# Moving the small updates of a top-k search and of the softmax sums from VectorE to GpSimd inside an attention stage

## The chip, the cores and the metric

The kernel runs on one core of a Trainium2 chip. The metric is the device time of one execution in microseconds (us), the median of three runs. The engines are named as the profile names them: PE (TensorE, matmul), PEld (its weight load), DVE (VectorE), ACT (ScalarE), POOL (GpSimd) and SP (SyncE, which here only issues DMAs). Each engine executes its own queue in order, and engines wait for each other through semaphores.

## The reference, cut to what matters

Two transformer-like layers on x of shape (4, 32, 32, 384). The change lies in the attention of layer 0:

```python
attn = softmax(einsum('bhnd,bhmd->bhnm', q, k) * scale)      # 4 x 12 heads, 1024 x 1024
gidx = argmax(einsum('bhnd,hgd->bhng', q, gp))               # 48 groups a head
q_mean = mean of q over the tokens of each group             # b h 48 32
qmw_t = einsum('bhgd,bhnd->bhgn', q_mean, k)
mask = the 96 largest of the 1024 values of each row of qmw_t
col = mask.sum(axis=2)                                       # how many groups chose token m
attn = attn * col[..., None, :]
attn = attn / (attn.sum(axis=2, keepdims=True) + 1e-08)      # normalised over the queries
out = einsum('bhnm,bhmd->bhnd', attn, v) @ proj_w.T
```

So a head needs, for each query n, the inverse of its sum of exponentials; for each key m, `col`; and then a second normalisation along the other axis. After attention come an expert feed-forward, a local attention and a second feed-forward, which the change does not touch.

## The kernel before, in words

All of attention is written as one loop over `step` (L889), with four steps to a head and 48 heads, 192 steps and ten more to drain. A step handles two of the eight blocks of 128 keys. The order of instructions on PE, DVE, ACT and SP is the order of the Python text; on POOL, which is not in that list, the compiler's scheduler chooses the order. Stages of one head are spread over steps:

- `scores(u)` (L649): four pairs of matmuls of a 32-row `k4` block with `q4` into two PSUM tiles `ps_s` (two buffers, so the next step's scores wait for this step's `exps`).
- `exps` (L659, ACT): two exponentials of 128 x 1024 to SBUF tiles `e`.
- `total(u)`, one step later (L667, `ps_z`): sums of exponentials over the keys, by matmul with ones.
- `gather`, when a head's four steps are over: ACT copies the sums (L681), SP writes them to DRAM (L683) and reads them back as `zz`, 128 x 2 x 8 (L685).
- `spread`, in step 1 of the next head: DVE adds the two halves (L693) and takes the reciprocal (L695); SP writes that to DRAM (L697) and reads it back repeated over all partitions as `rz` (L699). For the last head of an image three more DVE instructions (L703 to L705) check that the sums lie within bounds.
- `share(u)`, `SHARE` = 7 steps after the scores (L711, DVE): two instructions of 128 x 1024 multiply `e` by `rz` and by `inv` and sum along the row; then L716 and L718 make the scaled values `wv`.
- `out(u)`, `OUT` = 8 steps after the scores (L667, `ps_o`): the product with `wv`. `keep` copies it to SBUF (ACT, L731) and sends it to its place in `q`: SP writes one half (L740), POOL adds the other by an accumulating DMA (L738).
- `Head(n + 1)` is created in step 0 of head n and at once issues eight DMAs on POOL's queue, L636 and L637 in turn, that fill `q4` and `k4` (two buffers each).

Between these, `prepared` puts projections and grouping of the next image on PE, `project` and `residue` put the output projection of the image before, and `search` runs the top-k search. A search (`topk`, 20 tiles of up to 128 rows, two of them at a time) finds a bound by iteration: ACT counts how many of the 1024 values lie above the bound with a Sign and a running sum (L384 for the first size, then L391 eight times), and between two counts DVE makes the new bound from the count (L395, L397). After the last, DVE negates it (L401) and takes the largest values below (L404 to L425). Sign writes its unneeded output into `junk`, which is the same memory as `below`, the tile that L404 writes. A search advances by one part each time `search()` is called, twice in a step, after `share` and `spread`.

`residue` (L764, SP) loads the input row block that the output projection is added to, into `o`, a tile with one buffer until attention is over; L782 adds, L783 to L786 take statistics, L787 stores.

Of the kernel before, what the change touches and what calls it, by code (L numbers as in the profile page):

```python
# [10 lines left out]
FP = mybir.dt.float32  # L11
BF = mybir.dt.bfloat16
AF = mybir.ActivationFunctionType
ALU = mybir.AluOpType
# [3 lines left out]
P = 128  # L18
B, IMG, C = 4, 32, 384
NTOK = IMG * IMG  # L20
NB = NTOK // P
# [16 lines left out]
FIRST_BOUND, NEAR, SLOPE = 1.65, 92, 0.00366  # L38
DAMP = (0.9, 0.7, 0.5, 0.4, 0.3, 0.25, 0.2)
# [137 lines left out]
def attention(net, outer, router, x, x1, unsafe, qkv_wT, gpT, proj_wT, proj_w, gate_w, gate_b):  # L177
# [14 lines left out]
    tc, nc = net.tc, net.nc  # L192
    NHEAD = B * NH
# [6 lines left out]
    few = outer.enter_context(tc.tile_pool(name="at_few", bufs=2))  # L200
    psum = router.psum
    with ExitStack() as ctx:

        early = ctx.enter_context(tc.tile_pool(name="at_early", bufs=1))
        const = ctx.enter_context(tc.tile_pool(name="at_const", bufs=1))
# [3 lines left out]
        tiny = ctx.enter_context(tc.tile_pool(name="at_tiny", bufs=4))  # L209
# [40 lines left out]
        for t in range(5):  # L250
            for n in range(4):
                one = hsel[:, t, n : n + 1]
                lo = NG * (FIRST[t] + n) - P * t
                nc.gpsimd.affine_select(
                    out=one, in_=one, compare_op=ALU.is_ge, fill=0.0,
                    base=-lo, pattern=[[0, 1]], channel_multiplier=1,
                )
                nc.gpsimd.affine_select(
                    out=one, in_=one, compare_op=ALU.is_ge, fill=0.0,
                    base=lo + NG - 1, pattern=[[0, 1]], channel_multiplier=-1,  # L260
                )
        ones16 = const.tile([P, TOPK], BF, name="ones16")
        nc.gpsimd.memset(ones16, 1.0)
        nc.gpsimd.memset(qmbd, 0.0)
# [9 lines left out]
        nc.gpsimd.memset(topped[:, 0, :], 1.0)  # L274
        nc.gpsimd.memset(topped[:, 1, :], float(2 * TOPK - NTOK))
        below = const.tile([P, 512], FP, name="below")
        junk = below.bitcast(mybir.dt.bfloat16)
        fit = const.tile([P, B], FP, name="fit")
        onehot = const.tile([P, B * KC * NB // 2], FP, name="onehot")
        sums = lasting.tile([P, NE], FP, name="sums")  # L280
# [44 lines left out]
        reached, heads, projected, valued = set(), [], set(), set()  # L325
# [38 lines left out]
        def topk(b, t):  # L364
# [10 lines left out]
            n = rows_of(t)  # L375
            left = load(b, t)
            yield
            size = small("tk_size")
            parts = tiny.tile([P, 51], FP, name="tk_parts", tag="tk_parts", bufs=2)
            step, place, last, none, between = (parts[:, c : c + 1] for c in range(5))  # L380
# [3 lines left out]
            nc.scalar.activation(junk[:n], left[:n], AF.Abs, accum_out=size[:n])  # L384
            yield
            bound = small("tk_bound")
            nc.vector.tensor_scalar(bound[:n], size[:n], -FIRST_BOUND / NTOK, None, ALU.mult)
            for turn in range(len(DAMP) + 1):
                yield
                over = small("tk_over")  # L390
                nc.scalar.activation(junk[:n], left[:n], AF.Sign, bias=bound[:n], accum_out=over[:n])  # L391
                yield
                if turn == len(DAMP):
                    break
                nc.vector.scalar_tensor_tensor(step[:n], over[:n], float(NTOK - 2 * NEAR), size[:n], ALU.add, ALU.mult)  # L395
                old, bound = bound, small("tk_bound")
                nc.vector.scalar_tensor_tensor(  # L397
                    bound[:n], step[:n], -SLOPE * DAMP[turn] / NTOK, old[:n], ALU.mult, ALU.add
                )
            edge = best[:, 0:1]  # L400
            nc.vector.tensor_scalar(edge[:n], bound[:n], -1.0, None, ALU.mult)  # L401
            for half in range(2):
                cols = slice(half * 512, half * 512 + 512)
                nc.vector.scalar_tensor_tensor(  # L404
# [216 lines left out]
        class Head:  # L621
            def __init__(self, n):
                self.n, self.b, self.h = n, n // NH, n % NH
                self.c, self.j = self.h // 4, self.h % 4
                self.rows = slice(32 * self.j, 32 * self.j + 32)
                self.im = images[self.b]
                assert (self.b, self.c, "qk") in reached

                self.q4 = big.tile([P, 512], FP, name="q4", tag="q4", bufs=2)
                self.k4 = big.tile([P, 512], FP, name="k4", tag="k4", bufs=2)  # L630
                q = self.im["q"][self.c][self.rows, :]
                k = self.im["k"][self.c][self.rows, :].rearrange("p (a e t) -> p a e t", e=2, t=P)
                for r in range(4):
                    rows_ = slice(32 * r, 32 * r + 32)
                    odd, half = divmod(r, 2)
                    nc.gpsimd.dma_start(out=self.q4[rows_, :], in_=q[:, 512 * half : 512 * half + 512])  # L636
                    nc.gpsimd.dma_start(  # L637
                        out=self.k4[rows_, :].rearrange("p (a t) -> p a t", t=P), in_=k[:, :, odd, :]
                    )
                self.es = []  # L640
                self.s = tiny.tile([P, NB], FP, name="s", tag="s")

            def scores(self, u):
                self.ps = []
# [45 lines left out]
            def spread(self):  # L690

                z = self.im["z"][:, self.h, :]
                nc.vector.tensor_tensor(z, self.zz[:, 0, :], self.zz[:, 1, :], ALU.add)  # L693
                rr = tiny.tile([P, NB], FP, name="rr", tag="rr", bufs=2)
                nc.vector.reciprocal(rr, z)  # L695
                there = rows.tile([NTOK], FP, name="r_row", tag="r_row")
                nc.sync.dma_start(out=there.rearrange("(p i) -> p i", i=NB), in_=rr)  # L697
                self.rz = work.tile([P, NTOK], FP, name="rz", tag="rz")
                nc.sync.dma_start(out=self.rz, in_=there.partition_broadcast(P))  # L699
                if self.h == NH - 1:  # L700
                    every = self.im["z"].rearrange("p h i -> p (h i)")
                    n = NH * NB
                    nc.vector.tensor_scalar(below[:, :n], every, ZMAX, None, ALU.is_le)  # L703
                    nc.vector.tensor_scalar(below[:, n : 2 * n], every, 1 / ZMAX, None, ALU.is_ge)
                    nc.vector.tensor_reduce(fit[:, self.b : self.b + 1], below[:, : 2 * n], AX.X, ALU.min)  # L705
# [51 lines left out]
        def residue(b, t):  # L757
            if late:
                o = late[0].tile([P, C], FP, name="o", tag="o", bufs=2)
            else:  # L760
                o = few.tile([P, C], FP, name="o", tag="o", bufs=1)
            residues[b, t] = o
            r = b * NTOK + t * P
            nc.sync.dma_start(out=o, in_=x[r : r + P, :])  # L764
# [81 lines left out]
        def search():  # L846

            for one in list(searching):
                if next(one, 0) == 0:
                    searching.remove(one)  # L850
# [25 lines left out]
        for step in range(-AHEAD, 0):  # L876
# [8 lines left out]
                search()  # L885
            end()
        heads.append(Head(0))
        goal = spent
        for step in range(STEPS + OUT + 2):  # L889
            n, u = divmod(step, PAIRS)  # L890
            if n < NHEAD:
                heads[n].scores(u)
            if n < NHEAD:
                heads[n].exps()
            if 0 <= step - OUT < STEPS:
                heads[(step - OUT) // PAIRS].out((step - OUT) % PAIRS)
            if 0 <= step - 1 < STEPS:
                heads[(step - 1) // PAIRS].total((step - 1) % PAIRS)
            if u == 0 and 0 < n <= NHEAD:
                heads[n - 1].gather()  # L900
            if u == 0 and n + 1 < NHEAD:
                heads.append(Head(n + 1))
            if 0 <= step - OUT < STEPS:
                if (step - OUT) % PAIRS == PAIRS - 1:
                    heads[(step - OUT) // PAIRS].keep()
            b, i = divmod(step, PAIRS * NH)
            goal = min(goal + (RAMP if step < 12 else PACE), spent + MOST)
            begin(step)
            if step < 12:
                search()  # L910
                search()
            widen(step)
            o, t = i - OUT - 2, (i - OUT - 2) // 2
            if b and 0 <= o < 2 * NB and o % 2 == 0:
                project(b - 1, t)
            if b and o > 2 * NB:
                next(routing[b - 1], None)
            if b < B:
                for t in {3: [0], 4: [1, 2], 5: [3], 6: [4], 7: [5, 6], 8: [7]}.get(i, []):
                    value(b, t)  # L920
            while spent < goal and prepared():
                pass
            if zeros and step >= 4:
                zeros.pop(0)()
            if 0 <= step - SHARE < STEPS:
                heads[(step - SHARE) // PAIRS].share((step - SHARE) % PAIRS)
            if u == 1 and 0 < n <= NHEAD:
                heads[n - 1].spread()
            if b and 0 <= o + 1 < 2 * NB and o % 2:
                residue(b - 1, t + 1)  # L930
            search()
            end()
            search()
        residue(B - 1, 0)
        assert not ends and not others
        assert pending == [None, None] and begun == len(tiles) and not searching and not zeros
# [1529 lines left out]
```

## Time and profile before

| | us |
|---|---|
| median of three runs | 2756.25 (2753.23 to 2764.23) |
| profiled execution, its own time | 2774.66 |
| its span | 2772.8 |
| first and last exponential (L659) start | 83.7 and 1190.2 |
| DVE busy in the span | 1747.2 |
| PE busy in the span | 2550.5 |
| POOL busy in the span | 621.8 |

A row of the groups reads: line, engine, operation, what it writes `<-` what it reads, shapes, count; then busy time and mean duration in ns; then the idle time of the engine just before these instructions, and what ended most of that. A row of the waits reads: engine, tile and line that waited `<-` what it waited for: total, number of waits, longest. A row of the windows gives for each stretch the busy time of each engine, the number of instructions, the granted TensorE clock as a share of full speed, the DMA share and GB/s.

### The profile page before, as it was taken

The page shows a single profiled execution, that of the slowest core. Times are in us where ns is not written, and L with a number is a line of the kernel's source. Part 1 is how long each engine was busy: PE and PEld are TensorE (multiplying, and loading weights), DVE is VectorE, ACT ScalarE, POOL GpSimd, SP SyncE. Part 2 cuts the span into 40 slices and gives each one's busy share as a digit, 9 for nine tenths or more (in the row PEclk, how much of TensorE's full clock was granted, in tenths as well). Part 3 has the DMA queues.
Part 4 walks back from the last instruction along what each step waited for, and adds up shares of the span by engine and source line. Part 5 has one row for each costly group of instructions (what it writes and reads, how often), then busy time and mean ns, then how long its engine had stood idle before and what let it go on. Part 6 is the DMA issues. An engine that isn't in the chain of part 4 may idle for free. (4 is left out here: it accounts for less than half of the span.)

```text
span 2772.8 us, 40194 instructions
## 1 busy us (share of the span) xinstructions
PE 2550.5 (92%) x14667; PEld 1551.5 (56%) x14667; DVE 1747.2 (63%) x4490; ACT 1272.3 (46%) x2086; POOL 621.8 (22%) x885
## 2 busy tenths in 40 slices
PE   6879998989898998679999999999999998999988
PEld 3323332333233332137889999999899974555532
DVE  2367777777777778656625445554565457898962
ACT  3768776768676877421222112211111213456455
POOL 2112322242225223513221111222222111110000
PEclk9989998999999998779999999999999999999999
DMA  5133434322332233445475455566556536665532
GB/s 109 39 95 93 100 98 120 101 55 63 88 83 53 66 90 84 126 132 193 164 290 199 170 205 205 199 225 231 201 206 227 213 121 217 200 213 178 178 110 93
DMA packets 191231, 404.14 MB, mean 146 GB/s; under 512 B 83344, under 2 KB 152272, under 8 KB 177968
## 3 DMA queue, kind: packets, MB, share of 16 engines
q0 software_dynamic: 39248, 234.24, 25.6%
q1 hardware_dynamic: 142064, 156.33, 18.0%
q10 hardware_dynamic: 9712, 10.91, 1.3%
q8 instruction: 118, 1.93, 0.3%
q14 instruction: 89, 0.73, 0.1%
HBM read 304.34 MB, written 49.00 MB: 127 GB/s over the span
## 5 line engine op out<-in xcount | busy, mean ns | idle before, releaser
L1728 ACT ACTIVATE h<-ps_h,up 128x256 f32<-128x256 f32 (+1 forms) x420 | 194.9, 465 | 831.5 <-PE ps_h L1723 819.1
L1723 PE MATMUL ps_h<-xbT,up 128*128 128x256 f32 (+1 forms) x2520 | 533.9, 372 | 6.2 <-ACT h L1728 5.5
L1723 PEld LDWEIGHTS ps_h<-xbT,up 128*128 128x128 f32 x2520 | 464.2, 191 | 69.5 <-ACT h L1728 6.7
L711 DVE CUSTOM_DVE_ANT_0 e<-e,rz,inv 128x1024 f32<-128x1024 f32 x384 | 475.2, 1274 | 24.8 <-DMA rz<-r_row 24.8
L659 ACT ACTIVATE e<-ps_s,ten 128x1024 f32<-128x1024 f32 x384 | 407.8, 1108 | 83.9 <-PE ps_o L667 35.2
L649 PE MATMUL ps_s<-q,k 32*128 32x512 f32 x1536 | 278.8, 666 | 43.5 <-ACT e L659 41.5
L667 PE MATMUL ps_o<-e,wv 128*32 128x512 f32 x1536 | 228.2, 669 | 70.3 <-DVE wv L718 45.5
L636 POOL DMA_DIRECT2D q<-q x192 | 98.5, 514 | 640.4 <-PE ps_s L649 582.9
L667 PE MATMUL ps_z<-e,rt_ones 128*32 128x512 f32 x1536 | 218.3, 641 | 0.0
L391 ACT ACTIVATE below<-tk_left,tk_bound 128x1024 bf16<-128x1024 f32 (+1 forms) x160 | 184.2, 1151 | 63.8 <-DVE tk_bound L397 51.6
L1767 PE MATMUL ps_y<-wsum,hsum 128*128 128x192 f32 x1116 | 194.8, 327 | 6.8 <-DVE y L1771 5.0
L1767 PEld LDWEIGHTS ps_y<-wsum,hsum 128*128 128x128 f32 x1116 | 181.1, 190 | 10.7 <-DVE y L1771 7.7
L649 PEld LDWEIGHTS ps_s<-q,k 32*128 32x128 f32 x1536 | 84.1, 188 | 175.8 <-ACT e L659 104.5
L1907 PE MATMUL ps_a<-wa,xnT 128*128 128x486 f32 x384 | 162.4, 572 | 1.8 <-ACT xnT L174 1.8
L667 PEld LDWEIGHTS ps_o<-e,wv 128*32 128x32 f32 x1536 | 32.0, 112 | 231.0 <-issue 104.3
L1771 DVE TENSOR_TENSOR y<-ps_y,y 128x192 f32<-128x192 f32 x155 | 55.5, 358 | 166.8 <-PE ps_y L1767 159.8
L1567 POOL DMA_INDIRECT yt<-yg,index x64 | 78.5, 1227 | 358.9 <-DVE x L1870 164.8
L306 PE MATMUL ps_t<-xnT,wqkv 128*128 128x512 f32 x288 | 136.5, 615 | 3.3 <-ACT xnT L488 2.6
L637 POOL DMA_DIRECT2D k<-k x192 | 125.7, 655 | 10.1 <-issue 6.8
L667 PEld LDWEIGHTS ps_z<-e,rt_ones 128*32 128x32 f32 x1536 | 53.1, 118 | 131.7 <-issue 129.4
L1767 PE MATMUL ps_y<-down,h 128*128 128x192 f32 x744 | 126.0, 326 | 0.0
L1767 PEld LDWEIGHTS ps_y<-down,h 128*128 128x128 f32 x744 | 122.6, 190 | 1.6
(405 smaller groups left out, 3743.2 us busy)
## 6 DMA issues: line engine op xcount, KB each, us to landing
band<-room SPq DMA_DIRECT2D x32, 1560.0 KB
rz<-r_row SPq DMA_DIRECT2D x48, 512.0 KB
yg<-y SPq DMA_DIRECT2D x67, 192.0 KB
q<-q POOLq DMA_DIRECT2D x192, 64.0 KB
k<-k POOLq DMA_DIRECT2D x192, 64.0 KB
room<-none SPq DMA_DIRECT2D x64, 192.0 KB
x<-x SPq DMA_DIRECT2D x34, 192.0 KB
o<-in_x_dram SPq DMA_DIRECT2D x33, 192.0 KB
```

Of the source, the lines that this page charges most:

```text
L306: nc.tensor.matmul(ps, lhsT=lhsT(k), rhs=rhs(k), start=k == 0, stop=k == KC - 1)
L391: nc.scalar.activation(junk[:n], left[:n], AF.Sign, bias=bound[:n], accum_out=over[:n])
L636: nc.gpsimd.dma_start(out=self.q4[rows_, :], in_=q[:, 512 * half : 512 * half + 512])
L637: nc.gpsimd.dma_start(out=self.k4[rows_, :].rearrange("p (a t) -> p a t", t=P), in_=k[:, :, odd, :])
L649: nc.tensor.matmul(ps[:, half * 512 : half * 512 + 512], lhsT=self.k4[r, u * P : (u + 1) * P], rhs=self.q4[r, :], start=True, stop=True,)
L659: nc.scalar.activation(e, ps, AF.Exp, bias=shift, scale=QK_SCALE)
L667: nc.tensor.matmul(ps[r : r + 32, :], lhsT=lhsT(odd), rhs=self.es[2 * u + odd][:, half * 512 : half * 512 + 512], start=u == 0, stop=u == ...
L711: nc.vector.tensor_tensor_reduce(self.es[m], self.es[m], self.rz, 1.0, self.im["inv"][:, m, self.h : self.h + 1], ALU.mult, ALU.add, self. ...
L1723: nc.tensor.matmul(ps, lhsT=up[:, o : o + P], rhs=xbT[:, k, :size], start=k == 0, stop=k == KC - 1,)
L1728: nc.scalar.activation(hs[f // 3][:, f % 3, :size], ps, AF.Gelu, bias=up[:, KC * HID + f : KC * HID + f + 1])
L1767: nc.tensor.matmul(ps, lhsT=left[f], rhs=right[:, f, :], start=f == 0, stop=f == HF - 1)
L1907: nc.tensor.matmul(pa[:, :HW_], lhsT=xnTs[i][:, k, :], rhs=wa[:, k, hh * HW_ : (hh + 1) * HW_], start=k == 0, stop=k == KC - 1,)
```

## The change

Five edits in attention:

1. The search's small updates go from DVE to POOL: the first bound, the two instructions of a turn (as `tensor_scalar` with two operations, in place of `scalar_tensor_tensor`), and the negated bound. The largest-value part stays on DVE.
2. `spread`'s sum and inverse go to POOL. The inverse is a power of -1 followed by one Newton step: five instructions in place of two. The check of the bounds goes into `bound`, called two steps later.
3. The eight row loads of a head are issued three after step 0, three after step 1 and two after step 2, at the end of the step, in place of all eight at step 0.
4. `junk` gets memory of its own; `o` gets two buffers.
5. `dynamic_dma_scratch_size`, the memory for descriptors of POOL's DMAs, goes from 8192 to 4096.

```diff
+        minus = const.tile([P, NB], FP, name="minus")
+        nc.gpsimd.memset(minus, -1.0)
...
-        junk = below.bitcast(mybir.dt.bfloat16)
+        junk = const.tile([P, NTOK], BF, name="junk")
...
-            nc.vector.tensor_scalar(bound[:n], size[:n], -FIRST_BOUND / NTOK, None, ALU.mult)
+            nc.gpsimd.tensor_scalar(bound[:n], size[:n], -FIRST_BOUND / NTOK, None, ALU.mult)
+            edge = best[:, 0:1]
...
-                nc.vector.scalar_tensor_tensor(step[:n], over[:n], float(NTOK - 2 * NEAR), size[:n], ALU.add, ALU.mult)
+                nc.gpsimd.tensor_scalar(step[:n], over[:n], float(NTOK - 2 * NEAR), size[:n], ALU.add, ALU.mult)
                 old, bound = bound, small("tk_bound")
-                nc.vector.scalar_tensor_tensor(
+                nc.gpsimd.tensor_scalar(
                     bound[:n], step[:n], -SLOPE * DAMP[turn] / NTOK, old[:n], ALU.mult, ALU.add
                 )
-            edge = best[:, 0:1]
-            nc.vector.tensor_scalar(edge[:n], bound[:n], -1.0, None, ALU.mult)
+                if turn == len(DAMP) - 1:
+                    nc.gpsimd.tensor_scalar(edge[:n], bound[:n], -1.0, None, ALU.mult)
...
+            def load(self):
...
                     nc.gpsimd.dma_start(out=self.q4[rows_, :], in_=q[:, 512 * half : 512 * half + 512])
+                    yield
                     nc.gpsimd.dma_start(
                         out=self.k4[rows_, :].rearrange("p (a t) -> p a t", t=P), in_=k[:, :, odd, :]
                     )
+                    yield
...
-                nc.vector.tensor_tensor(z, self.zz[:, 0, :], self.zz[:, 1, :], ALU.add)
-                rr = tiny.tile([P, NB], FP, name="rr", tag="rr", bufs=2)
-                nc.vector.reciprocal(rr, z)
+                nc.gpsimd.tensor_tensor(z, self.zz[:, 0, :], self.zz[:, 1, :], ALU.add)
+                rr, t = (tiny.tile([P, NB], FP, name=name, tag=name, bufs=2) for name in ("rr", "rr_t"))
+                nc.gpsimd.tensor_tensor(rr, z, minus[:, :NB], ALU.pow)
+                nc.gpsimd.tensor_tensor(t, z, rr, ALU.mult)
+                nc.gpsimd.tensor_scalar(t, t, -1.0, 2.0, ALU.mult, ALU.add)
+                nc.gpsimd.tensor_tensor(rr, rr, t, ALU.mult)
...
+            def bound(self):
+
                 if self.h == NH - 1:
...
-                o = few.tile([P, C], FP, name="o", tag="o", bufs=1)
+                o = few.tile([P, C], FP, name="o", tag="o")
...
             if u == 0 and n + 1 < NHEAD:
                 heads.append(Head(n + 1))
+                loads = heads[-1].load()
...
+            if u == 3 and 0 < n <= NHEAD:
+                heads[n - 1].bound()
...
             search()
             end()
             search()
+            for _ in range(3 if u < 3 else 0):
+                next(loads, None)
...
-    nc = bacc.Bacc("TRN2", target_bir_lowering=False, num_devices=1, dynamic_dma_scratch_size=8192)
+    nc = bacc.Bacc("TRN2", target_bir_lowering=False, num_devices=1, dynamic_dma_scratch_size=4096)
```

More of the change, by code (lines that the diff above doesn't have):

```diff
@@ L630, in __init__ @@
                 self.k4 = big.tile([P, 512], FP, name="k4", tag="k4", bufs=2)
+                self.es = []
+                self.s = tiny.tile([P, NB], FP, name="s", tag="s")
+            def load(self):
                 q = self.im["q"][self.c][self.rows, :]
@@ L639, in __init__ @@
                     )
-                self.es = []
-                self.s = tiny.tile([P, NB], FP, name="s", tag="s")
+                    yield
             def scores(self, u):
@@ L887, in attention @@
         heads.append(Head(0))
+        for _ in heads[0].load():
+            pass
         goal = spent
```

## The prediction

> **What bounds the kernel now.** I read the page's slices for the stage, then windows of that stage, then the waits of each engine in it, then the rows of the instructions that move.
>
> ```profile
> PE   6879998989898998679999999999999998999988
> DVE  2367777777777778656625445554565457898962
> ...
> core 0: us, PE busy (x) PEld busy (x) DVE busy (x) ACT busy (x) POOL busy (x), PEclk, DMA share, GB/s
> 80.00:140.00 60.00, 52.70 (x322) 20.62 (x320) 20.34 (x73) 45.52 (x81) 8.46 (x16) 0.91 0.18 47
> 140.00:1120.00 980.00, 885.14 (x5790) 307.35 (x5790) 734.86 (x2192) 714.24 (x1097) 286.97 (x464) 0.94 0.33 85
> 1120.00:1240.00 120.00, 78.00 (x421) 27.71 (x422) 72.13 (x202) 36.64 (x43) 50.01 (x52) 0.74 0.38 117
> ```
>
> A slice is 69 us; attention is slices 2 to 18. In its long middle (140 to 1120 us) PE is busy for 885 of 980 us, DVE for 735, ACT for 714. So PE bounds it, and the most that easier going on other engines can bring there is PE's idle time, 95 us, with 7 us ahead of it and 42 us in the tail. The question is who causes these idle times:
>
> ```profile
> PE ps_o L667 <- DVE wv L718: 45.5, 18, 11.8
> PE ps_s L649 <- ACT e L659: 41.5, 21, 4.2
> PE ps_o L667 <- DVE tk_parts L395: 19.7, 8, 3.7
> PE ps_t L487 <- DVE gate_o L783: 10.0, 5, 3.1
> ...
> DVE tk_parts L395 <- ACT below L391: 81.6, 43, 7.5
> DVE zall L693 <- DMA zz<-z_row: 43.1, 23, 4.1
> ...
> ACT below L391 <- DVE tk_bound L397: 51.6, 27, 6.2
> ...
> POOL q L636 <- PE ps_s L649: 582.9, 41, 54.0
> POOL q L738 <- DMA q<-po: 98.0, 38, 15.8
> ```
>
> These are the waits of the window 60 to 1270 us. PE waits for DVE's `wv` (L395 named as releaser is the same wait: the two stand next to each other in DVE's queue) and for ACT's exponentials. DVE in its turn stands still at the head of its queue for 81.6 us until ACT has counted, and for 43.1 us until a sum has come back from DRAM, with `share` instructions behind it that could run. ACT stands 51.6 us for DVE's new bound, with exponentials behind it. The search thus ties the two queues together, and PE pays at the end.
>
> ```profile
> L711 DVE CUSTOM_DVE_ANT_0 e<-e,rz,inv 128x1024 f32<-128x1024 f32 x384 | 475.2, 1274 | 24.8 <-DMA rz<-r_row 24.8
> L397 DVE SCALAR_TENSOR_TENSOR tk_bound<-tk_parts,tk_bound 128x1 f32<-128x1 f32 (+1 forms) x140 | 22.1, 158 | 5.0
> L395 DVE SCALAR_TENSOR_TENSOR tk_parts<-tk_over,tk_size 128x1 f32<-128x1 f32 (+1 forms) x140 | 20.5, 146 | 81.7 <-ACT below L391 81.6
> L695 DVE RECIPROCAL rr<-zall 128x8 f32<-128x8 f32 x48 | 9.8, 203 | 1.7
> L258 POOL TENSOR_SCALAR_AFFINE_SELECT hsel<-hsel 128x1 bf16<-128x1 bf16 x20 | 2.6, 179 | 0.0
> ```
>
> **The change part by part.** All sums are against the profiled execution's own 2774.66 us, which is 18.4 us (0.7%) above the median of 2756.25; the difference is carried over to the median.
>
> *Off DVE.* Instructions: 20 of L387 (151 ns), 140 each of L395 and L397 (146 and 158), 20 of L401 (135), 48 each of L693 and L695 (164 and 203): 3.0 + 20.5 + 22.1 + 2.7 + 7.9 + 9.8 = 66 us of busy time. Idle time that goes with them: 81.6 (L395) + 17.5 (L387) + 43.1 (L693) = 142 us. The separate `junk` frees L404 from ACT's Sign on the same memory: 20.0 us of L404's idle time were such waits. With two buffers for `o`, the load of the next block no longer waits for the store of this one: L782 waited 30.4 us for it, 19.6 of them outside the tail, where there are two buffers already.
>
> None of this is time of the kernel by itself; it counts where PE waited for DVE: 45.5 + 19.7 + 10.0, and 5.1 of a wait on L401, together 80.3 us. The tail (1115 to 1270 us) holds 32.3 of it, where the last heads wait for `rz` and no search is left; this stays. Of the other 48 us I take 60% as gone: −29. Not all, because some come behind work that stays: in the timeline at 148.5 us PE has waited 4.2 us, and DVE had spent the 5 us before on layer-norm statistics and `share`.
>
> *Onto POOL.* 320 search instructions (16 a tile) and 240 of `spread`. No row of the trace has POOL doing arithmetic on two operands. The nearest is the affine select on 128x1, 179 ns; DVE's own 146 to 203 ns are of the same size. I take 0.2 us for each, 112 us in all; POOL is busy for 287 of 980 us in the middle, so it stays under half. For the power there is no near row; bounds are 0.2 us (the reciprocal on DVE) and 1.2 us (POOL's longest row, the indirect DMA); I take 0.6.
>
> *The lock.* The rows show 475 us of L711, an instruction with two SBUF inputs, in about half of attention's time. The Trainium skill, "SBUF — State Buffer", section "Who interferes with whom", says that such a DVE instruction and a GpSimd instruction that reads SBUF exclude each other, each for its whole length, and "Perfetto Trace Analysis", section "Optimizing Scalar/DVE Operations", warns that moving work between the two may therefore not help. No row of before has a POOL instruction that reads SBUF beside L711; the DMA issues beside it are steady (L637 551 to 1240 ns, median 558). By the rows alone an update takes 2 x 0.2 us. By the rule, each of its two instructions finds L711 running half the time, with 0.64 us of its 1.27 us to go on average, and the second can meet a whole L711 that got in between: 0.4 + 0.3 + 0.6 + some 0.1 for semaphores, 1.4 us from count to bound. From the trace, the median from the end of ACT's count to the end of L397 is 1.5 us today, since DVE gets to it late. So even by the rule the new bound comes no later in the middle case, and ACT has a pair of exponentials (2.1 us) between most counts. The reverse hold, L711 waiting for POOL, is at most 560 x 0.2 us x one half = 56 us of DVE, less than the 66 us it was relieved of. I go with the rule here; by the rows alone the new bound would nearly always be in time, and the next term −25 in place of −12.
>
> *ACT.* Its waits on the bound, 51.6 us plus 12 us put down to neighbours of L397, I take as halved: −31 us of ACT's idle time. ACT waited some 100 us for DVE in all and PE 41.5 us for exponentials, 0.4 us for each; −12.
>
> *The chain of a head.* `zz` to `rr` takes 0.4 us on DVE. On POOL: four instructions at 0.2 us, the power 0.6, and about 0.4 us of lock for each: some 3 us, less what DVE came late to `zz`. SP's L697 waits longer for it, and behind it in SP's queue stand L740, L764 and L787. From the issue of L699 to the first L711 of that head the trace has a median of 5.6 us over the heads, and 3.4 us when DVE waits for it, so 2.2 us are free. About half of the heads come late by a us or so: 25 us of DVE idle time. PE uses that `wv` a step later, about 5 us, so I book +5, and +2 for the last head in the tail, where nothing covers.
>
> *Behind what an update queues.* POOL stands 582.9 us at L636 until PE has freed `q4`, and 98.0 us at L738 until the first half of `keep` has landed; an update behind it waits too. The first is harmless: PE's scores of that step precede the ACT work that the update serves. The second is 2.6 us a time, 38 times, so about one update in ten meets it: +3. The loads are issued up to two steps (10 us) later. From a head's last load issue to its first scores the trace has 11 to 23 us for nearly all heads, so they land in time: 0; without that cover each head would wait for a landing of about 3 us (as `rz` takes), 48 times.
>
> *Scratch and `bound`.* No POOL row shows a wait for descriptor memory; the 19.1 us of "issue" in front of L1400 are the nearest. Doubled, and none of it hidden, +19; nothing, 0. It cannot gain. I take 0, as PE is at nine tenths in the stage that follows. `bound` moves three cheap instructions: 0.
>
> *Clock.* The granted clock is 1.00 in 70 us windows with PE 69 us busy and 0.88 to 0.90 in those with 59; fewer gaps should return a little: −4.
>
> Sum: −29 − 12 + 5 + 2 + 3 − 4 = −35 us. 2774.66 − 35 = 2740, and at the median 2756.25 − 35 = 2721.
>
> **The rivals.**
> 1. *POOL becomes the pacemaker of the search* (slower). If an update on POOL takes over 3 us from count to bound, be it by slow instructions, the lock, or loads ahead of it, then it exceeds the 2.1 us of exponentials, and ACT waits at almost each of the 140 turns. At 1.2 us a turn that is 168 us of ACT waits in place of 63: +105 x 0.4 = +42 on PE, with DVE's relief of −29 partly lost as its share waits for late `rz`: net +30, 2786. For it: the lock rule, two dependent instructions a turn, and POOL's queue that stands so often. Against: today's DVE path is 1.5 us too, and small POOL instructions are 0.1 to 0.2 us in every row.
> 2. *No change to speak of.* PE's idle time is 10% and the DVE waits are moved, not removed: `rz` late by 3 us puts DVE's idle time back, and the gain on PE is −10: 2746. For it: the margin of `rz` is only 2.2 us. Against: the relief of L395's 81.6 us does not depend on `rz`.
> 3. *The ties loosen more than I count.* PE's "busy" time also holds waits inside groups of matmuls (scores of 2.1 us in place of 1.1 when the second PSUM tile was not free), so PE's idle time understates the gain: −65, 2691.
>
> **How the numbers follow.** Forecast 45% (2705 to 2738), rival 1 22%, rival 2 18%, rival 3 15%. 0.5% of 2756 is 14 us, about what a measurement of this kernel can tell from no change. Faster by more: forecast and rival 3 and a little of rival 2, 0.62; same: most of rival 2, 0.16; slower: rival 1, 0.22. The range runs from 2688, the middle of rival 3, to 2782, close to the middle of rival 1, so that about a fifth lies outside.
>
> **What would show it.** Right: L395's 81.6 us gone from DVE's waits, and zz's 43.1; PE's waits on `wv` outside the tail under 25 us; L391's wait on POOL under 35 us; POOL's small rows near 0.2 us. Lock: those POOL rows at 0.5 us or more, or L711 above 1274 ns. Chain: DVE's wait on `rz` in the middle above today's 6.7 us. Wrong: ACT's wait for the bound above 100 us, or PE's for DMA `k`; or a gain outside 80 to 1240 us.

## The result: 3.1% slower, and the profile after

| | before | after |
|---|---|---|
| median of 4 runs, us | 2754.74 (2744.97 to 2764.23) | 2836.54 (2831.04 to 2838.23) |
| span of the profiled execution, us | 2772.8 | 2834.9 |
| first and last exponential start, us | 83.7, 1191.6 | 83.8, 1253.0 |
| mean granted clock | 0.958 | 0.948 |

The ratio after to before is 1.0313 with a 95% interval of [1.0292, 1.0334] (the two medians alone give 1.0297); 2721 was forecast, 1.3% faster. (The 1190.2 us that stand in the table of before are the last exponential but one.) The stretch from the first to the last exponential grew by 61.3 us, the span by 62.1: all of the loss is in attention. (The profiled execution of before took 2774.66 us and lay above its median, so the medians differ by more, 82 us.)

In the changed kernel the lines are shifted: `share` is L725 (was L711), `wv` L732 (L718), the search's update L398 and L400 (L395, L397), ACT's count L394 (L391), the sum L701 (L693), the power L703, Newton's step L704 to L706, SP's store and reload L708 and L710 (L697, L699), exponentials L667 (L659), PE's helper L675 (L667). The page's slices and the windows of the changed kernel:

```profile
PE   6979898979898988658999999999999998999988
DVE  1267677756676767554734445455555557898962
POOL 2335654565446655731421111222222111110000
...
core 0: us, PE busy (x) PEld busy (x) DVE busy (x) ACT busy (x) POOL busy (x), PEclk, DMA share, GB/s
140.00:1120.00 980.00, 855.28 (x5564) 299.31 (x5565) 655.40 (x1708) 682.08 (x1051) 530.85 (x909) 0.92 0.32 81
1120.00:1240.00 120.00, 72.55 (x438) 19.87 (x438) 70.14 (x222) 54.42 (x67) 73.36 (x103) 0.77 0.34 97
```

In the same 980 us PE was busy for 885 us and is now for 855, and it did 5564 matmuls in place of 5790. POOL went from 287 to 531 us, far from full. No engine became a bound by its busy time; PE has more holes. The waits of the window 60 to 1350 us (engine, tile, line `<-` what it waited for: total, times, longest) say who makes them:

```profile
POOL tk_parts L398 <- ACT junk L394: 247.6, 86, 9.8
DVE e L725 <- DMA rz<-r_row: 174.4, 26, 20.4
...
PE ps_o L675 <- DVE wv L732: 117.0, 35, 19.7
ACT e L667 <- PE ps_o L675: 114.4, 29, 20.9
...
POOL zall L701 <- DMA zz<-z_row: 77.5, 31, 7.9
...
DVE g_max L580 <- PE ps_t L598: 69.5, 22, 19.0
...
PE ps_s L657 <- ACT e L667: 42.3, 19, 11.2
...
ACT junk L394 <- POOL tk_bound L400: 26.5, 22, 5.8
```

The search's waits did what was foreseen: DVE's 81.6 us at the update are gone (POOL stands there now, which harms little by itself: from SP's issue of `zz` to the start of the sum behind it pass 3.1 us in the mean, 2.9 before), DVE's 43.1 us for `zz` are gone, and ACT's wait for a bound fell from 51.6 to 26.5 us, plus 15.9 us for the first bound. But DVE's wait for `rz` rose from 24.8 to 174.4 us. (19.8 of these are at head 0, where nothing is lost by it: DVE comes to its first `share` early, and that one starts at 121.8 us, before at 127.0.) The same wait is passed on: PE's for `wv` went from 65.2 us (45.5, and 19.7 under L395's name) to 117.0, ACT's for the buffers that `ps_o` gives back from 35.2 to 114.4.

What POOL took, by groups with shapes kept apart, and one chain in the timeline (start, duration, engine and line, in brackets the idle time before it):

```profile
L725 DVE CUSTOM_DVE_ANT_0 e<-e,rz,inv 128x1024 f32<-128x1024 f32 x384 | 475.9, 1276 | 196.5 <-DMA rz<-r_row 174.4
L703 POOL TENSOR_TENSOR rr<-zall,minus 128x8 f32<-128x8 f32 x48 | 91.8, 1913 | 3.4
L398 POOL TENSOR_SCALAR tk_parts<-tk_over,tk_size 128x1 f32<-128x1 f32 x112 | 48.0, 428 | 209.9 <-ACT junk L394 209.4
L705 POOL TENSOR_SCALAR rr_t<-rr_t 128x8 f32<-128x8 f32 x48 | 24.9, 518 | 4.2
```
```profile
674.59 0.20 POOL L701 TENSOR_TENSOR zall<-zz 128x8 f32<-128x8 f32 x1 [1.16 <-DMA zz<-z_row]
674.87 1.68 POOL L703 TENSOR_TENSOR rr<-zall,minus 128x8 f32<-128x8 f32 x1
676.64 0.19 POOL L704 TENSOR_TENSOR rr_t<-zall,rr 128x8 f32<-128x8 f32 x1
676.90 1.19 DVE L725 CUSTOM_DVE_ANT_0 e<-e,rz,inv 128x1024 f32<-128x1024 f32 x1
676.92 1.23 POOL L705 TENSOR_SCALAR rr_t<-rr_t 128x8 f32<-128x8 f32 x1
...
678.01 1.28 DVE L725 CUSTOM_DVE_ANT_0 e<-e,rz,inv 128x1024 f32<-128x1024 f32 x1
678.23 1.13 POOL L706 TENSOR_TENSOR rr<-rr,rr_t 128x8 f32<-128x8 f32 x1
679.39 0.33 SPq L708 DMA_DIRECT2D r_row<-rr  x1
680.84 0.32 SPq L710 DMA_DIRECT2D rz<-r_row  x1
...
684.69 1.28 DVE L725 CUSTOM_DVE_ANT_0 e<-e,rz,inv 128x1024 f32<-128x1024 f32 x1 [3.48 <-DMA rz<-r_row]
```

The power alone takes 1.68 us here. L705 and L706 each begin while a `share` runs and end 0.06 us after it, 1.1 to 1.2 us for instructions that take 0.2 us alone (see the end). From the start of the sum to SP's store pass 4.8 us; DVE then stands 3.5 us for `rz`. Over all 48 heads that distance has a mean of 4.3 us, and was 0.4 in the kernel before.

### The profile page after: what moved, and what is told of

It is laid out like the page before. It is cut to its first block, busy times and chain, and to the rows that moved or that the text cites. A ratio compares the mean times of both kernels' runs of the same rounds, so it can differ in the third digit from the quotient of the medians.

```text
span 2834.9 us, 40531 instructions
## 1 busy us (share of the span) xinstructions
PE 2557.8 (90%) x14667; PEld 1555.9 (55%) x14667; DVE 1694.8 (60%) x4074; ACT 1273.3 (45%) x2086; POOL 920.7 (32%) x1446
## 5 line engine op out<-in xcount | busy, mean ns | idle before, releaser
L725 DVE CUSTOM_DVE_ANT_0 e<-e,rz,inv 128x1024 f32<-128x1024 f32 x384 | 475.9, 1276 | 196.5 <-DMA rz<-r_row 174.4
L667 ACT ACTIVATE e<-ps_s,ten 128x1024 f32<-128x1024 f32 x384 | 410.1, 1108 | 150.7 <-PE ps_o L675 114.4
L675 PE MATMUL ps_o<-e,wv 128*32 128x512 f32 x1536 | 232.7, 681 | 131.5 <-DVE wv L732 117.0
L675 PE MATMUL ps_z<-e,rt_ones 128*32 128x512 f32 x1536 | 224.4, 657 | 0.0
L394 ACT ACTIVATE junk<-tk_left,tk_bound 128x1024 bf16<-128x1024 f32 (+1 forms) x160 | 184.1, 1151 | 43.0 <-POOL tk_bound L400 26.5
L675 PEld LDWEIGHTS ps_o<-e,wv 128*32 128x32 f32 x1536 | 32.8, 114 | 292.9 <-issue 161.3
L657 PEld LDWEIGHTS ps_s<-q,k 32*128 32x128 f32 x1536 | 83.8, 192 | 172.4 <-ACT e L667 105.9
L398 POOL TENSOR_SCALAR tk_parts<-tk_over,tk_size 128x1 f32<-128x1 f32 (+1 forms) x140 | 62.2, 444 | 248.4 <-ACT junk L394 247.6
L1624 POOL DMA_INDIRECT up<-in_wup_dram,rows_w_all x31 | 34.1, 1101 | 294.0 <-ACT h L1749 271.3
L675 PEld LDWEIGHTS ps_z<-e,rt_ones 128*32 128x32 f32 x1536 | 54.5, 120 | 135.1 <-issue 133.1
```

Of the source, the lines that this page charges most:

```text
L657: nc.tensor.matmul(ps[:, half * 512 : half * 512 + 512], lhsT=self.k4[r, u * P : (u + 1) * P], rhs=self.q4[r, :], start=True, stop=True,)
L667: nc.scalar.activation(e, ps, AF.Exp, bias=shift, scale=QK_SCALE)
L675: nc.tensor.matmul(ps[r : r + 32, :], lhsT=lhsT(odd), rhs=self.es[2 * u + odd][:, half * 512 : half * 512 + 512], start=u == 0, stop=u == ...
L725: nc.vector.tensor_tensor_reduce(self.es[m], self.es[m], self.rz, 1.0, self.im["inv"][:, m, self.h : self.h + 1], ALU.mult, ALU.add, self. ...
```

## The experiments

The theory: `rz` comes later by these 3.8 us, and that alone is the loss. The rival was the forecast's rival 1: POOL as pacemaker of the search, or POOL beside DVE at all. A ratio is always to the kernel before, run beside it on the same chip.

**The two moves apart.** e1 puts the sum and inverse back on DVE, e2 the search's updates, e3 both; the loads in threes, the buffers, the later check of bounds and the smaller descriptor memory stay.

```diff
# e1; e3 has both edits
-                nc.gpsimd.tensor_tensor(z, self.zz[:, 0, :], self.zz[:, 1, :], ALU.add)
...
-                nc.gpsimd.tensor_tensor(rr, rr, t, ALU.mult)
+                nc.vector.tensor_tensor(z, self.zz[:, 0, :], self.zz[:, 1, :], ALU.add)
+                nc.vector.reciprocal(rr, z)
# e2
-                nc.gpsimd.tensor_scalar(step[:n], over[:n], ...)
+                nc.vector.scalar_tensor_tensor(step[:n], over[:n], ...)
```

> The changed kernel with the sum and its inverse back on DVE (two instructions); the search's updates stay on POOL, and loads, buffers and scratch stay as changed. Theory 1 (the inverse comes too late through POOL: 4.3 us from the sum's start to the row write in place of 0.4, DVE then waits 174 us for rz in place of 25): the loss of some 82 us goes, 2745 to 2760, or down to 2721 if moving the search brings what was forecast; DVE's wait for rz falls to about 25 us. Theory 2 (POOL is too slow for the search, ACT waits for bounds): stays at about 2830. Theory 3 (the loads, the buffers or the smaller scratch cost it): stays at about 2830.

> The changed kernel with the search's updates back on DVE; the sum and its inverse stay on POOL. Theory 1: stays slow, 2810 to 2840, DVE's wait for rz well above 100 us. Theory 2: back to 2750. Theory 3: stays at about 2830.

> Both groups back on DVE; what is left of the change are the loads three per step, junk of its own, two buffers for o, the later check of bounds and the smaller scratch. Theories 1 and 2: 2740 to 2755, a little under before thanks to the buffers. Theory 3: about 2830.

| | median us | ratio | DVE's wait for `rz`, us |
|---|---|---|---|
| e1, search on POOL | 2757.59 | 1.0037 [1.0022, 1.0053] | 38.1 |
| e2, sum on POOL | 2838.46 | 1.0330 [1.0296, 1.0363] | 133.5 |
| e3, neither | 2737.06 | 0.9964 [0.9950, 0.9978] | 17.9 |

The loss goes with the sum, not with the search: e2 is as slow as the whole change, and e1 is free of nearly all of it. Rival 1 is refuted. By the quotients of the ratios the sum on POOL costs 1.0313/1.0037, 2.75% or 76 us beside the search on POOL, and 1.0330/0.9964, 3.7% or 101 us, without it.

But the search on POOL brings nothing either: e1 lies 0.7% above e3. The waits of e1, then those of e3, show where DVE's relief went:

```profile
DVE zall L701 <- DMA zz<-z_row: 94.1, 29, 10.9
...
PE ps_o L675 <- DVE wv L729: 65.9, 28, 5.1
...
DVE g_max L580 <- PE ps_t L598: 50.6, 19, 17.4
...
DVE col L460 <- PE ps_t L444: 39.4, 12, 8.9
...
DVE e L722 <- DMA rz<-r_row: 38.1, 18, 5.9
```
```profile
DVE tk_parts L398 <- ACT junk L394: 80.3, 43, 7.6
...
DVE zall L701 <- DMA zz<-z_row: 51.9, 23, 5.9
...
PE ps_o L675 <- DVE wv L729: 48.4, 20, 5.1
...
PE ps_o L675 <- DVE tk_parts L398: 19.4, 8, 3.2
DVE col L460 <- PE ps_t L444: 16.9, 10, 4.1
DVE e L722 <- DMA rz<-r_row: 17.9, 9, 3.6
DVE g_max L580 <- PE ps_t L598: 12.4, 11, 1.8
```

Without the 80.3 us at the update, DVE stands at the next thing in its queue: 42 us more for `zz`, 38 for `g_max`, 23 for `col`, 20 for `rz`, 123 us together. PE's waits for `wv` are the same, 65.9 us against 48.4 + 19.4. DVE's wait at the update had been slack in front of inputs that were not there yet.

**The dose.** e4 leaves Newton's step out (L704 to L706; the inverse is then the bare power). e7 is e3, all on DVE, with two more copies of the 4 KB row through DRAM before `rz` is read: `rz` is late with POOL out of the chain. e11 and f11 have one copy.

```diff
# e4
-                nc.gpsimd.tensor_tensor(t, z, rr, ALU.mult)
-                nc.gpsimd.tensor_scalar(t, t, -1.0, 2.0, ALU.mult, ALU.add)
-                nc.gpsimd.tensor_tensor(rr, rr, t, ALU.mult)
# e7, on e3; range(1) in e11 and f11
+                for hop in range(2):
+                    again = rows.tile([NTOK], FP, name=f"r_row{hop}", tag=f"r_row{hop}")
+                    nc.sync.dma_start(out=again.rearrange(...), in_=there.rearrange(...))
+                    there = again
```

> The changed kernel without the Newton step on the inverse (three of the five instructions of the chain left out, so the inverse is POOL's bare power): the chain is shorter by 54 us over 48 heads, 1.1 us each. Theory 1: of the 82 us about a fifth to a third comes back, 2810 to 2820, and DVE's wait for rz falls by 30 to 50 us. Theories 2 and 3: no change, 2836.

> The kernel with both groups on DVE (2737 us), and two more copies from DRAM to DRAM, on SP's queue, between the row of inverses and its broadcast, so that rz comes some 3.5 to 4 us later with nothing on POOL. If lateness of rz is the whole cause: slower by 60 to 80 us, about 2805, with DVE's wait for rz above 100 us. If what costs is POOL's part itself (the port lock, its queue): within 10 us of 2737.

> Both groups on DVE and one more copy from DRAM to DRAM in front of the broadcast in place of two. Two made 4.0 us of lateness a head and 95 us (ratio 0.9964 to 1.0309). Linear from the start, with no slack: 2.0 us and 45 to 50 us, ratio 1.013 to 1.015. If there is slack of about 2 us, as the prediction assumed: under 15 us, ratio below 1.002.

> One extra copy in front of the broadcast, beside the kernel with both on DVE. Linear without slack: 1.7% above it (two copies: 3.45%). With slack in the first 2 us: under 0.5% above it.

| pair | `rz` later by, us | quotient of ratios | us | us per us |
|---|---|---|---|---|
| f11 (1.0069 [1.0044, 1.0094]) to f3 (0.9946) | 2.3 | 1.0124 | 34 | 15 |
| e7 (1.0309 [1.0282, 1.0336]) to e3 (0.9964) | 4.1 | 1.0346 | 95 | 23 |
| e2 (1.0330) to e3 (0.9964) | 3.7 | 1.0367 | 101 | 27 |
| after (1.0313) to e4 (1.0177 [1.0151, 1.0204]) | 1.6 | 1.0134 | 37 | 23 |
| after (1.0313) to e1 (1.0037) | 3.8 | 1.0275 | 76 | 20 |

The delays are differences of means over the heads of sum to store, or of store to reload. e11 was slower too, 1.0095 [1.0065, 1.0125], on another chip without e3 beside it; f11 and f3 repeat the pair side by side on one chip. The last two rows are the roughest: the changed kernel ran beside neither e4 nor e1, and one kernel's ratio can move by 0.8%, 23 us, between chips (e1 and f1, below). e4 gave back more than the fifth to a third that was expected, with DVE's wait for `rz` down by 41 us to 133.4. With nothing of it on POOL, e7 has the loss of the whole change (95 us, where 60 to 80 were expected):

```profile
DVE e L726 <- DMA rz<-r_row: 123.0, 28, 14.7
PE ps_o L675 <- DVE wv L733: 83.1, 24, 11.9
PE ps_o L675 <- DVE tk_parts L398: 62.7, 17, 9.1
```

e7 is best laid beside e2, which has the search on DVE too and its late sum on POOL. DVE waits 133.5 us for `rz` there and 123.0 here, PE for DVE 153.7 and 145.8 us, and the ratios are 1.0330 and 1.0309. So a late row is enough, whoever causes it. A us of it costs 15 to 27 us, a third to over a half of a us in each of 48 heads, and already the first two us cost. f11 lies between its two expectations: its first 2.3 us cost less per us than the next two do (e7).

One thing these runs do not separate. The row goes by SP's queue, and while SP stands at its store or its reload, the loads of `residue` behind it stand too: DVE's wait for the row block `o` (L796; L793 in e3, L797 in e7) is 32.7 us in e3 and 54.9 in e7, 30.4 in before and 63.0 in after. PE's own wait for what follows from `o` is small (10.0 us before, 16.4 after, 2.0 in e7), but what these DVE waits hold up behind them is not measured. No run delays `rz` without SP's queue.

**Buffers and loads.** e8 is the kernel before with `junk` of its own, two buffers for `o` and the smaller descriptor memory only.

```diff
-        junk = below.bitcast(mybir.dt.bfloat16)
+        junk = const.tile([P, NTOK], BF, name="junk")
-                o = few.tile([P, C], FP, name="o", tag="o", bufs=1)
+                o = few.tile([P, C], FP, name="o", tag="o")
-    nc = bacc.Bacc(..., dynamic_dma_scratch_size=8192)
+    nc = bacc.Bacc(..., dynamic_dma_scratch_size=4096)
```

> The kernel before with junk in its own memory, two buffers for o and the scratch of 4096; loads, search and sum as before. If the buffers make the 10 us by which the kernel with both groups on DVE is faster than before: about 2737. If the loads three per step make it: about 2747, as before.

2748.29, 0.9984 [0.9969, 0.9999]: at most 0.3% of gain. e3 has the loads and the later check besides and stands at 0.9964 [0.9950, 0.9978]; the two intervals overlap, so that the loads bring anything (0.2% by the ratios) is not shown.

**POOL's queue at an image's end.** In the changed kernel the longest waits for `rz` after head 0's are at heads 20, 32 and 44, 13.5, 17.2 and 20.4 us. Its timeline at head 20:

```profile
605.47 0.97 POOL L1421 DMA_INDIRECT table<-rt_ge,rt_there  x1 [0.30 <-issue]
606.46 0.21 POOL L701 TENSOR_TENSOR zall<-zz 128x8 f32<-128x8 f32 x1
606.85 0.98 POOL L1421 DMA_INDIRECT table<-rt_ge,rt_there  x1 [0.18 <-issue]
607.84 1.71 POOL L703 TENSOR_TENSOR rr<-zall,minus 128x8 f32<-128x8 f32 x1
609.75 1.03 POOL L1421 DMA_INDIRECT table<-rt_ge,rt_there  x1 [0.20 <-issue]
...
611.62 0.33 SPq L708 DMA_DIRECT2D r_row<-rr  x1
611.94 1.15 ACT L394 ACTIVATE junk<-tk_left,tk_bound 128x1024 bf16<-128x1024 f32 x1 [8.43 <-POOL tk_bound L389]
616.92 1.28 DVE L725 CUSTOM_DVE_ANT_0 e<-e,rz,inv 128x1024 f32<-128x1024 f32 x1 [13.50 <-DMA rz<-r_row]
```

The router's scatters (L1421), some 1.28 us from one to the next, stand ahead of the sum and between its instructions, and ahead of ACT's first bound too. e5 (on e1) and e6 (on the change) meant to spread them over the steps; e9 and e10 do the same and also make each scatter's data in its own step.

```diff
# e5, e6; e9, e10 too
-            if t % 2 == 0:
+            if t % 2 == 0 or b < B - 1:
# e9, e10 only
+            if b < B - 1:
+                for n, value in enumerate((mean, rs)):
+                    nc.vector.tensor_copy(ids.bitcast(FP)[:, t, 1 + n : 2 + n], value[:, t : t + 1])
```

> The kernel with the search on POOL and the sum on DVE (2757.6 us), and the router's 16 scatters of an image (indirect DMAs of 1.2 us on POOL's queue) issued two in a step in place of four, for the three images routed inside the loop. Theory A (the search on POOL costs 20 us against the kernel with both on DVE because three times some 20 us of scatters stand ahead of its updates): 2738 to 2748, and the two quarters of the loop that hold scatters, 153 and 145 us for 24 steps, come down to about 142 and 137. Rival B (DVE's waits only moved to the next instruction in its queue, and the updates on POOL are late everywhere): 2757, no change.

> The changed kernel with the same wider spacing of the scatters. Theory 1 (late rz, linear in its lateness): DVE's waits for rz at heads 20, 32 and 44, which were 13.5, 17.2 and 20.4 us, fall to under 6 each, and the time by 25 to 35 us, to about 2805. Rival (those waits are covered or come back elsewhere): no change, 2836.

> The changed kernel, with the scatters of an image really spread: the two small copies that fill the scattered rows are made per row block on DVE, one block in a step, so that POOL cannot have its scatters ready earlier (the spacing by text alone had left POOL's order as it was). Theory 1: DVE's waits for rz at heads 20, 32 and 44 (13.5, 17.2, 20.4 us) fall to about 5, and the time by 25 to 35 us against the changed kernel, to a ratio of about 1.02. Rival: those waits cost little, since something else is as late there: ratio 1.03.

> The same spreading in the kernel with the search on POOL and the sum on DVE (ratio 1.0037 to before). Theory A: the scatters ahead of the search's updates made its 20 us against the kernel with both on DVE (0.9964): ratio 0.997 to 1.000. Rival B: ratio 1.003 to 1.004.

e5 (2765.75, 1.0038 [1.0022, 1.0053]) and e6 (2848.12, 1.0330 [1.0303, 1.0356]) left POOL's order as it was, since the compiler sets that: they test nothing. In e9 the scatters are apart, and the waits at heads 20, 32 and 44 fell to 0, 3.5 and 3.4 us; but those one head later rose from 4.4, 3.2 and 13.3 to 6.5, 9.0 and 17.0, others rose elsewhere (at heads 8, 24, 36 and 46 by some 7 us each), and all waits for `rz` stayed at 171.0 us. e9 took 2832.35, 1.0216 [1.0184, 1.0247]; e10, 2757.44, 0.9952 [0.9923, 0.9981]. By its ratio alone e9 would fit theory 1, which said about 1.02; but e10 lies about as far below e1 on that same other chip, and DVE's waits did not fall. The quotient e9 to e10, 1.0265, is close to that of after to e1, 1.0275: the sum on POOL costs the same with the scatters out of its way.

**One chip for all.** The kernel before took 2746.79 us beside e1 to e4 and 2755.01 beside e5 to e8, both on one chip, and 2769.86 beside e9 to e11 on another. f1, f3, f10 and f11 are e1, e3, e10 and e11 again, side by side on a third chip (before there: 2781.26):

> Search on POOL, sum on DVE, on the same chip as the spread scatters. If the order of chips carries over: ratio 1.004, some 0.7% above both on DVE. If the 0.9% between it and the spread scatters was the chip: equal to the kernel with spread scatters.

> Both groups on DVE, once more, so that the three kernels beside it have it on their own chip: ratio 0.996, as measured.

> Search on POOL, sum on DVE, scatters really spread, now beside its two neighbours. Theory A (scatters ahead of the updates made the loss): at least 0.5% under the kernel without the spreading, and equal to both on DVE. Rival B: no difference to the kernel without, since its 24 steps with the first scatters took 152.0 us in place of 153.4 only; the better ratio came from the other chip, where before took 2770 us.

f1 2767.91, 0.9953 [0.9936, 0.9970]; f3 2765.90, 0.9946 [0.9929, 0.9963]; f10 2759.36, 0.9935 [0.9913, 0.9957]. The search on POOL neither gains nor loses here (f1 to f3), where it lost 0.7% on the other chip; a gain shows on neither. Whether spreading the scatters helps e1 (f10 to f1, 0.2% with overlapping intervals) stays open. With both groups on DVE the kernel is faster than before on both chips, by 0.4 and 0.5% (e3, f3).

## Why the prediction was wrong, by its steps

- *The chain of a head, +5 and +2.* This step failed, and decides the sign. Its size was too small: the power was taken at 0.6 us, between bounds of 0.2 and 1.2, and measured 1.67 alone, 1.91 in the mean; the chain was put at 3 us and measured 4.3. Its price was far too small. "2.2 us are free" took the median over heads for a margin, and set against it the 3.4 us of the quickest head; the eight heads at which DVE waited in before have a median of 3.9, and 31 of the 48 heads had less than 2.2 us in hand above that. Then 25 us of DVE's wait were turned into 5 us of PE, a fifth. In f11 DVE's wait for `rz` is 64.8 us and in f3 23.9, and for these 41 us more the kernel is 34 us slower. At f11's 15 us per us the forecast's own 2.6 us later (3 less 0.4) would have been +39; with the measured 3.8 us it was +76. The tail, booked at +2, is part of it: by the starts of the exponentials in the profiled executions, the changed kernel is 51 us behind e1 when head 44 begins and 81 us at the last `wv`, so 30 us came in the last four heads (f11 to f3: 24 and 35, so 12).
- *Off DVE, −29.* The waits went as said (81.6 and 43.1 us), the gain did not come: e1 against e3 is +0.7% on one chip, +0.1% on the other. It counted PE's waits for DVE as caused by DVE's waits at the update, but what followed in DVE's queue was not ready either. The sign that it named for this, PE's waits for `wv` under 25 us outside the tail, did not come: they are 51.1 us from 140 to 1120 us, against 38.0 before. And the wait for the block `o` was no matter of its one buffer: with two it is 29.4 us in e8, 30.4 before.
- *ACT, −12.* ACT's waits for bounds fell by a third (63 to 42 us), not by half; PE's wait for exponentials stayed at 42 us (41.5 before). In e1 they fell by more than half, to 27.7 us, and PE's wait was 43.4: no gain either way.
- *Onto POOL and the lock.* Right, in sign and size: by the trace an update's instruction takes 0.26 us, or 0.9 to 1.1 with `share` running, and from the end of a count to the end of the new bound pass 1.3 us in the median, where 1.4 was worked out. So the rule that was followed, "SBUF — State Buffer", "Who interferes with whom" in the Trainium skill, holds in this trace for the POOL side. The reverse hold did not show: L725 takes 1276 ns, L711 took 1274, and 16 `share` instructions that began in the middle of a power took 1266 ns in the mean.
- *Behind what an update queues, +3.* The accumulating DMA's wait was no issue (98.0 us before, 49.2 after); the scatters ahead of the sum and of a first bound were not seen at all. What they cost by themselves is open: e9 moved the waits to other heads and did not remove them.
- *Scratch, loads and `bound`, 0.* In accord with e8 and e3: together with the buffers, −0.4%.
- *Clock, −4.* Of the other sign: fewer matmuls per us, and a granted clock of 0.92 in place of 0.94 in the middle. (Of the windows with 59 us that it read at 0.88 to 0.90, one, 560 to 630 us, had 0.93.)
- *The rivals.* Rival 1 came closest in its number and is refuted by e2. Rival 2 named the mechanism ("`rz` late by 3 us puts DVE's idle time back") but put the whole at a gain of 10 us, where that mechanism alone cost 76. The sign that was set for it, DVE's wait for `rz` in the middle above 6.7 us, came: 102.9.

By quotients the terms are: buffers −0.16% (e8), loads and check −0.2% (e3 to e8), search +0.7% (e1 to e3), sum +2.75% (after to e1); that they come to the 3.1% is by construction. The order matters: by way of e2 the sum is +3.7% and the search then −0.2%. It fits that a late `rz` also holds up the bounds while DVE makes them (ACT waits 80.7 us for L400's bound in e2, 54.3 in e3).

Why a late `rz` costs so much is argued from the waits and not proved by a run of its own: `share` stands at the head of DVE's queue, `wv` follows it, PE's `ps_o` waits for `wv`, and only `ps_o` frees the `e` buffers for ACT's next exponentials and so for the next head's sum (35.2 to 114.4 us for ACT). In e7 that last wait rose less, to 51.3 us, while PE's for DVE rose from 67.8 (e3) to 145.8, so the share of each link differs. A `share` one step later, which would give `rz` more room, was not tried.

## What to carry to other kernels

Before moving a small instruction to an idle engine, find the chain that it stands in: on a chain whose end the bottleneck waits for, latency is the price, and the median slack of it is no margin. Delay that chain by a known amount with as little else changed as can be (here an extra copy through DRAM) and read off the us per us. And a wait at the head of a queue is worth only what stands behind it and is ready: removing it moves the engine to its next wait.

## What of the hardware was not expected

- POOL's power on 128x8 took 1662 to 2610 ns, eight times DVE's reciprocal of the same shape (203 ns).
- POOL instructions of 0.20 to 0.26 us took 0.9 to 1.1 us when a `share` was running at their start (L398 0.89, L400 1.10, L705 1.10, medians), and ended some 0.1 us after it (0.13, 0.13 and 0.06). L389, with one input of 128x1 and constants only, is no exception, although its medians are alike (0.23 and 0.22): all six that met a `share` ended 0.08 to 0.17 us after it, but four of them met only its last tenth of a us; the one that met 1.08 us of it took 1.16. The row loads' DMA issues were not held (0.52 us both ways).
- The kernel before, unchanged, had medians of 2747 to 2781 us on three chips, 1.2% apart, and kernels do not move alike: e1 and f1 are one kernel, 1.0037 and 0.9953. Differences under 1% need both kernels on one chip.
